# A graph attention layer's edge loop: one-hots turned on TensorE, score parts summed on VectorE, and steps staggered over three groups

## The chip, the cores and the metric

The kernel runs on one core of one Trainium2 chip. Its engines work side by side: TensorE (PE; its weight loads are listed apart as PEld), VectorE (DVE), ScalarE (ACT), GpSimd (POOL) and SyncE (SP), and 16 DMA engines. Engines wait for one another through semaphores. SBUF is the working memory, PSUM the memory into which TensorE writes.

The metric is the device time of one execution in microseconds (us). "Clock" is the share of full speed that the throttle granted to TensorE.

## The reference, cut to what matters

Four graph layers follow one another over 4096 nodes of 512 features and 65536 edges. The change touches the first, an attention layer with 8 heads:

```python
h = jnp.einsum('nc,hcf->hnf', x, W)
# ... s_src, s_dst: one number per node and head, from h
e = s_src[:, :, None] + s_dst[:, None, :]
e = jnp.where(e > 0, e, ALPHA * e)              # 0.2 * e where negative
e = jnp.where(adj[None, :, :], e, NEG_INF)      # only along edges, and from a node to itself
att = jax.nn.softmax(e, axis=-1)
out = jnp.einsum('hij,hjf->hif', att, h)
return jax.nn.softmax(out.transpose(1, 0, 2).reshape(N, H * F), axis=1)
```

## The kernel before

Edges are sorted by source node and cut into 544 tiles of 128 edges; a pair of tiles belongs to one block of 128 source nodes. Eight tiles are a group, and the loop does one group a step, 68 steps. Per group:

- GpSimd gathers, tile by tile, the row of each edge's far node: 512 features and 8 scores.
- A one-hot matrix `oh` (edge by node of the block) adds weighted rows up: `oh.T @ rows` on TensorE, two tiles into one PSUM tile `sum_ps`, which VectorE adds to `acc` ("keep").
- The turned one-hot `oh_t` (node by edge) brings each edge the numbers of its source node. They are split into three bf16 parts, so that three bf16 products add up to an f32 value in `e_ps`.

In the kernel before, the places of the edges were written to DRAM during the sort, broadcast back to all partitions by a DMA, and VectorE made `oh_t` by comparing them with the partition's number:

```python
def fetch(g):
    rows = ep.tile([P, GT, DA], F32, name="rows", bufs=4)
    for j in range(GT):
        gather(rows[:, j, :D + H], htab, s_dst[:, at(g) + j:at(g) + j + 1])
    return rows

def source_parts(g, places):
    oh_t = ep.tile([P, GT * P], BF16, name="oh_t")
    nc.vector.tensor_scalar(oh_t, places, col_i, None, op0=OP.is_equal)
    e_ps = eps.tile([P, GT, 2, H], F32, name="e_ps")
    # ... ScalarE copies the node parts of four blocks into `of`
    for j in range(GT):
        for k in range(3):
            nc.tensor.matmul(e_ps[:, j]..., oh_t[:, j * P:(j + 1) * P], of[:, j // 2, k, :],
                             start=k == 0, stop=k == 2)
    return e_ps

def weigh(j, rows):                    # two of eight heads on ScalarE, six on VectorE
    two = rows[:, j:j + 2]
    # ... ScalarE: heads VH.. of both tiles
    g = two[:, :, :VH * F].rearrange("p t (h f) -> p t h f", h=VH)
    nc.vector.tensor_mul(g, g, two[:, :, D:D + VH].unsqueeze(3).to_broadcast([P, 2, VH, F]))

for g in range(-3, groups):            # order of issue, on every engine (checks at both ends left out)
    # fetch(g + 3); fetch_places(g + 2)
    e_ps = source_parts(g + 1, places.pop(g + 1))
    ps = None
    for j in range(0, GT, 2):
        weigh(j, rows[g])
        if ps is not None:
            keep(g, j - 2, ps)
        ps = add_up(g, j, rows[g], done[g])
        if j == 2:
            u = scores(rows[g + 1], e_ps)
    done[g + 1] = weights(g + 1, rows[g + 1], u)      # also makes the one-hots
    keep(g, GT - 2, ps)
```

Both operands of `weigh` on VectorE lie in SBUF, and so do both operands of the one-hots (a row of numbers and the places `s_loc`).

## Time and profile before

Median 6524.48 us (6512.19 to 6527.41, 3 runs). The edge loop runs from 277.5 to 1048.4 us.

| In the loop, 300 to 1030 us | busy us | share of 730 us |
|---|---|---|
| TensorE | 581 | 80% |
| VectorE | 570 | 78% |
| GpSimd | 569 | 78% |
| ScalarE | 325 | 45% |
| DMA engines, mean | | 75% |

For GpSimd "busy" is the issuing of a gather, 1.080 us in the mean; the rows land later (median 3.8 us from issue to landing). One more line of the kernel before, from the view of VectorE's waits in the same stretch (engine, line, waited for: us in total, times, longest):

```profile
DVE u L707 <- DMA rows<-htab,s_dst: 4.3, 5, 2.4
```

VectorE, which takes the scores of the next group as soon as its rows have landed, waits for a landing 5 times in 66 steps.

### The profile page before, as it was taken

To read this page: it belongs to the slowest core of one execution; us is meant where nothing else is said; L and a number is where in the kernel's file an instruction comes from. 1 tells how busy PE (TensorE), PEld (TensorE's weight loads), DVE (VectorE), ACT (ScalarE), POOL (GpSimd) and SP (SyncE) were. 2 spreads that over 40 slices of the span, in tenths; PEclk is the share of its full clock that TensorE was granted. 3 is DMA by queue.
4 is the path that set the end of the run, shared out by engine and by line. 5 is a ranking of instruction groups with operands and counts; after the bars stand their busy time and mean duration, and the time that the engine had idled before them with its cause. 6 is when DMAs were issued, how large, how long until landed. Compare 5 with 4: busy or idle time off the path is not lost. (4 is left out here: it accounts for less than half of the span.)

```text
span 6523.0 us, 65629 instructions
## 1 busy us (share of the span) xinstructions
PE 5718.0 (88%) x18462; PEld 2778.4 (43%) x18462; DVE 4141.7 (63%) x7141; ACT 2937.3 (45%) x3977; POOL 3254.1 (50%) x3324
## 2 busy tenths in 40 slices
PE   6678887888779799999999999999999889978885
PEld 4366664322224344444444444444444365532221
DVE  7577778455443376676676776776766545556665
ACT  3244444300011277777777777777777533300001
POOL 1277772477760365555555555555555100037774
PEclk9899999999899899999999999999999899989998
DMA  8777775566774333333333333333333211137777
GB/s 225 182 220 214 218 215 176 162 201 203 195 214 175 125 109 103 102 98 104 101 98 105 101 98 102 103 98 106 100 98 104 82 45 62 59 106 209 210 209 243
DMA packets 399757, 926.39 MB, mean 142 GB/s; under 512 B 135926, under 2 KB 135926, under 8 KB 399382
## 3 DMA queue, kind: packets, MB, share of 16 engines
q0 software_dynamic: 230976, 721.66, 37.6%
q1 hardware_dynamic: 168406, 200.39, 9.6%
q8 instruction: 155, 2.54, 0.2%
q14 instruction: 220, 1.80, 0.1%
HBM read 818.71 MB, written 103.11 MB: 141 GB/s over the span
## 5 line engine op out<-in xcount | busy, mean ns | idle before, releaser
L438 PE MATMUL m_ps<-w_sb,h_t 128*128 128x512 f32 x4224 | 1905.9, 599 | 31.2 <-ACT h_t L957 31.2
L803 PE MATMUL sum_ps<-g,oh 128*128 128x512 f32 x2144 | 1146.9, 636 | 218.1 <-DMA g<-ztab,d_src 80.2
L438 PEld LDWEIGHTS m_ps<-w_sb,h_t 128*128 128x128 f32 x4224 | 771.1, 190 | 983.6 <-issue 791.2
L449 POOL DMA_INDIRECT qg<-qtab,eg x528 | 504.0, 954 | 990.6 <-ACT h_t L957 845.7
L449 POOL DMA_INDIRECT g<-ztab,d_src x528 | 501.4, 950 | 866.4 <-issue 811.6
L459 DVE TENSOR_TENSOR acc<-acc,sum_ps 128x512 f32 x800 | 550.2, 688 | 546.4 <-PE sum_ps L803 541.4
L803 PEld LDWEIGHTS sum_ps<-g,oh 128*128 128x128 f32 x2144 | 336.9, 191 | 1015.4 <-DVE acc L459 388.5
L449 POOL DMA_INDIRECT g<-ytab,s_dst x544 | 536.9, 987 | 353.2 <-DMA ytab<-acc 185.6
L914 POOL DMA_INDIRECT eg<-aug,d_eid x528 | 569.0, 1078 | 242.4 <-issue 131.0
L449 POOL DMA_INDIRECT rows<-htab,s_dst x544 | 585.9, 1077 | 204.9 <-issue 138.9
L957 ACT COPY h_t<-tr_ps 128x512 f32<-128x512 f32 x528 | 283.6, 589 | 777.6 <-PE tr_ps L955 777.6
L735 PE MATMUL sum_ps<-rows,oh 128*128 128x261 f32 x2176 | 551.5, 410 | 60.3 <-PE sum_ps L735 41.2
L449 POOL DMA_INDIRECT pg<-ptab,eg x528 | 508.7, 963 | 160.9 <-issue 160.6
L735 PEld LDWEIGHTS sum_ps<-rows,oh 128*128 128x128 f32 x2176 | 427.3, 202 | 163.3 <-PE sum_ps L735 66.3
L967 PE MATMUL small_ps<-z,oh 128*128 128x512 f32 x1056 | 477.8, 595 | 8.4 <-DVE z L1027 8.4
L1006 DVE TENSOR_TENSOR z<-m_ps,b_bc 128x512 f32<-128x512 f32 x132 | 91.3, 692 | 467.3 <-PE m_ps L438 467.3
L459 DVE TENSOR_TENSOR acc<-acc,small_ps 128x512 f32 x528 | 361.1, 684 | 31.8 <-PE small_ps L967 4.3
L1165 ACT ACTIVATE acc<-acc,dis 128x512 f32<-128x512 f32 x32 | 19.7, 706 | 671.2 <-DVEq L464 671.2
L1027 DVE TENSOR_TENSOR z<-z,t 128x1024 f32<-128x1024 f32 x264 | 310.4, 1217 | 8.2 <-ACTq L464 4.8
L992 DVE TENSOR_TENSOR z<-m_ps,b_bc 128x512 f32<-128x512 f32 x132 | 91.3, 692 | 352.6 <-PE m_ps L438 352.6
L967 PEld LDWEIGHTS small_ps<-z,oh 128*128 128x128 f32 x1056 | 201.5, 191 | 263.7 <-issue 221.9
L955 PEld LDWEIGHTS tr_ps<-ident,pg 128*128 128x128 f32 x2112 | 248.0, 142 | 151.1 <-issue 120.0
(248 smaller groups left out, 8389.5 us busy)
## 6 DMA issues: line engine op xcount, KB each, us to landing
aug<-row SPq DMA_DIRECT2D x32, 560.0 KB, 3.9
places<-loc_rows SPq DMA_DIRECT2D x68, 256.0 KB, 3.8
xt<-in_x_dram SPq DMA_DIRECT2D x16, 1024.0 KB, 5.7
row<-in_edge_attr_dram SPq DMA_DIRECT2D x32, 512.0 KB, 6.6
x<-xt SPq DMA_DIRECT2D x16, 1024.0 KB, 4.3
xt<-x SPq DMA_DIRECT2D x16, 1024.0 KB, 7.5
rows<-htab,s_dst POOLq DMA_INDIRECT x544, 3.8
g<-ytab,s_dst POOLq DMA_INDIRECT x544, 3.7
```

The lines of the kernel that those rows point to most:

```text
L438: nc.tensor.matmul(ps, h_t[:, k, :], w_sb[:, k0 + k, :], start=start and k == 0, stop=stop and k == KC - 1)
L449: nc.gpsimd.indirect_dma_start(out=dst_ap, out_offset=None, in_=table, in_offset=bass.IndirectOffsetOnAxis(ap=idx, axis=0))
L459: nc.vector.tensor_add(into, into, ps)
L735: nc.tensor.matmul(ps[:, c, :HW], oh[:, j + k, :], rows[:, j + k, c * HW:(c + 1) * HW], start=k == 0, stop=k == 1)
L803: nc.tensor.matmul(ps, oh[:, j + k, :], g[:, j + k, :], start=k == 0, stop=k == pair - 1)
L914: nc.gpsimd.indirect_dma_start(out=eg[:, j // 2, (j % 2) * HALF:(j % 2 + 1) * HALF], out_offset=None, in_=aug.rearrange("e c -> (e c)").un ...
L955: nc.tensor.transpose(h_ps[:, k, :], h[:, j, k * P:(k + 1) * P], ident)
L957: nc.scalar.copy(h_t, h_ps)
L967: nc.tensor.matmul(ps, oh, m, start=True, stop=True)
L992: nc.vector.tensor_add(zz[:, 0, :], ps, b2_bc)
L1006: nc.vector.tensor_add(zz[:, 1, :], ps, b2_bc)
L1027: nc.vector.tensor_mul(mz[:, j:j + 2], mz[:, j:j + 2], t[:, j:j + 2])
```

## The change

The intent: no broadcast through DRAM and no comparison on VectorE; TensorE turns the one-hots that exist anyway; one product of 48 columns in place of three of 16 that accumulate; VectorE adds the three parts; and the work of a step is dealt out over three groups, so that no engine waits for a result that was only just begun.

```diff
-            def fetch_places(g): ...          # DMA broadcast of the places
+            def turn(oh):
+                made = []
+                for j in range(0, GT, 4):
+                    t_ps = eps.tile([P, 4, P], F32, name="t_ps")
+                    for k in range(4):
+                        nc.tensor.transpose(t_ps[:, k, :], oh[:, j + k, :], ident)
+                    made.append(t_ps)
+                return made
+            def turned(g, made):
+                oh_t = ep.tile([P, GT, P], BF16, name="oh_t")
+                for j, t_ps in enumerate(made):
+                    nc.scalar.copy(oh_t[:, 4 * j:4 * j + 4, :], t_ps)
                 ...
-                e_ps = eps.tile([P, GT, 2, H], F32, name="e_ps")
+                e_ps = eps.tile([P, GT, 3, 2 * H], F32, name="e_ps")
                 for j in range(GT):
-                    for k in range(3): nc.tensor.matmul(..., of[:, j // 2, k, :], start=k == 0, stop=k == 2)
+                    nc.tensor.matmul(..., of[:, j // 2].rearrange("p k c -> p (k c)"), start=True, stop=True)
             def scores(rows, e_ps):
+                near = ep.tile([P, GT, 2 * H], F32, name="near")
+                nc.vector.reduce_sum(near, e_ps.rearrange("p t k c -> p t c k"), axis=AX.X)
                 ...
+            # order of a step, with w = weigh, k = keep, a = add_up:
+            #   turn(g+1); w0; a0; w2; k6 of g-1; turned(g+1); a2; w4; k0; one_hots(g+2);
+            #   source_parts(g+1); a4; scores(g+1); w6; k2; a6; weights(g+1); k4
```

ScalarE's share of the weighing (`weigh_last`) became a function of its own and is issued one pair ahead. The one-hots get three buffers. Nothing else in the kernel is touched, but that the cast and the store of the places leave the sort.

More of the change, by code (lines that the diff above doesn't have):

```diff
@@ L86 @@
                    allow_small_or_imprecise_dtypes=True)
-    col_i = const.tile([P, 1], F32, name="col_i")
-    nc.gpsimd.iota(col_i, pattern=[[0, 1]], base=0, channel_multiplier=1,
-                   allow_small_or_imprecise_dtypes=True)
     acc = keep_pool.tile([P, NB, DA], F32, name="acc")
@@ L114 @@
     aug = dram.tile([E + 1, EA], F32, name="aug")
-    loc_rows = dram.tile([G * P, P], BF16, name="loc_rows")
     x1 = dram.tile([N, D], F32, name="x1")
@@ L305, in by_order @@
         placed(s_loc, loc)
-        low_p = pool.tile([P, G, P], BF16, name="low_p")
-        nc.vector.tensor_copy(low_p, loc)
-        nc.sync.dma_start(loc_rows.rearrange("(g p) c -> p g c", p=P), low_p)
         new = pool.tile([P, G, P], F32, name="new")
@@ L439, in product, with one_hots @@
                              start=start and k == 0, stop=stop and k == KC - 1)
-    def one_hots(pool, loc, t0, n):
-        oh = pool.tile([P, n, P], F32, name="oh")
+    def one_hots(pool, loc, t0, n, bufs=None):
+        oh = pool.tile([P, n, P], F32, name="oh", bufs=bufs)
         nc.vector.tensor_tensor(oh, row_i.unsqueeze(1).to_broadcast([P, n, P]),
@@ L683, in fetch @@
                 return rows
-            def fetch_places(g):
-                places = ep.tile([P, GT * P], BF16, name="places", bufs=3)
-                nc.sync.dma_start(places, loc_rows[at(g):at(g) + GT].rearrange("t c -> (t c)").partition_broadcast(P))
-                return places
-            def source_parts(g, places):
-                oh_t = ep.tile([P, GT * P], BF16, name="oh_t")
-                nc.vector.tensor_scalar(oh_t, places, col_i, None, op0=OP.is_equal)
-                e_ps = eps.tile([P, GT, 2, H], F32, name="e_ps")
+            def turn(oh):
[10 more added lines that the diff above has]
+                    nc.scalar.copy(oh_t[:, 4 * j:4 * j + 4, :], t_ps)
                 of = ep.tile([P, GT // 2, 3, 2 * H], BF16, name="of")
@@ L698, in source_parts @@
                     nc.scalar.copy(of[:, j // 2], node3[:, ds(b, 1)].rearrange("p b k c -> p (b k) c"))
+                return oh_t, of
+            def source_parts(oh_t, of):
+                e_ps = eps.tile([P, GT, 3, 2 * H], F32, name="e_ps")
                 for j in range(GT):
-                    for k in range(3):
-                        nc.tensor.matmul(e_ps[:, j].rearrange("p c h -> p (c h)"), oh_t[:, j * P:(j + 1) * P],
-                                         of[:, j // 2, k, :], start=k == 0, stop=k == 2)
+                    nc.tensor.matmul(e_ps[:, j].rearrange("p k c -> p (k c)"), oh_t[:, j, :],
+                                     of[:, j // 2].rearrange("p k c -> p (k c)"), start=True, stop=True)
                 return e_ps
             def scores(rows, e_ps):
+                near = ep.tile([P, GT, 2 * H], F32, name="near")
+                nc.vector.reduce_sum(near, e_ps.rearrange("p t k c -> p t c k"), axis=AX.X)
                 u = ep.tile([P, GT, H], F32, name="u")
-                nc.vector.tensor_add(u, e_ps[:, :, 0, :], rows[:, :, D:D + H])
+                nc.vector.tensor_add(u, near[:, :, :H], rows[:, :, D:D + H])
                 nc.vector.scalar_tensor_tensor(u, u, 0.2, u, op0=OP.mult, op1=OP.max)
-                nc.vector.tensor_sub(u, u, e_ps[:, :, 1, :])
+                nc.vector.tensor_sub(u, u, near[:, :, H:])
                 nc.vector.tensor_scalar(u, u, SAFE_RANGE + 10.0, None, op0=OP.min)
@@ L718, in weights, with weigh_last @@
                                      s_new[:, at(g):at(g) + GT].unsqueeze(2).to_broadcast([P, GT, H]))
-                return one_hots(ep, s_loc, at(g), GT)
-            def weigh(j, rows):
+            def weigh_last(j, rows):
                 two = rows[:, j:j + 2]
@@ L727, in weigh @@
                                              scale=two[:, k, D + h:D + h + 1])
+            def weigh(j, rows):
+                two = rows[:, j:j + 2]
                 g = two[:, :, :VH * F].rearrange("p t (h f) -> p t h f", h=VH)
@@ L742, in keep @@
                 nc.vector.tensor_add(into, into, ps[:, :, :HW])
-            rows, places, done = {}, {}, {}
-            for g in range(-3, groups):
+            rows, ohs, sums = {}, {}, {}
+            for g in range(-3, groups + 1):
                 now = lambda k: 0 <= k < groups
@@ L748, in run @@
                     rows[g + 3] = fetch(g + 3)
+                if now(g + 1):
+                    made = turn(ohs[g + 1])
+                if now(g):
+                    weigh(0, rows[g])
+                    sums[0] = add_up(g, 0, rows[g], ohs[g])
+                    weigh_last(2, rows[g])
+                    weigh(2, rows[g])
+                if now(g - 1):
+                    keep(g - 1, 6, sums.pop(6))
+                    del rows[g - 1], ohs[g - 1]
+                if now(g + 1):
+                    parts = turned(g + 1, made)
+                if now(g):
+                    sums[2] = add_up(g, 2, rows[g], ohs[g])
+                    weigh_last(4, rows[g])
+                    weigh(4, rows[g])
+                    keep(g, 0, sums.pop(0))
                 if now(g + 2):
-                    places[g + 2] = fetch_places(g + 2)
+                    ohs[g + 2] = one_hots(ep, s_loc, at(g + 2), GT, 3)
                 if now(g + 1):
-                    e_ps = source_parts(g + 1, places.pop(g + 1))
-                ps = None
-                for j in range(0, GT, 2):
-                    if now(g):
-                        weigh(j, rows[g])
-                        if ps is not None:
-                            keep(g, j - 2, ps)
-                        ps = add_up(g, j, rows[g], done[g])
-                    if j == 2 and now(g + 1):
-                        u = scores(rows[g + 1], e_ps)
+                    e_ps = source_parts(*parts)
+                if now(g):
+                    sums[4] = add_up(g, 4, rows[g], ohs[g])
                 if now(g + 1):
-                    done[g + 1] = weights(g + 1, rows[g + 1], u)
+                    u = scores(rows[g + 1], e_ps)
                 if now(g):
-                    keep(g, GT - 2, ps)
-                    del rows[g], done[g]
+                    weigh_last(6, rows[g])
+                    weigh(6, rows[g])
+                    keep(g, 2, sums.pop(2))
+                    sums[6] = add_up(g, 6, rows[g], ohs[g])
+                if now(g + 1):
+                    weights(g + 1, rows[g + 1], u)
+                    weigh_last(0, rows[g + 1])
+                if now(g):
+                    keep(g, 4, sums.pop(4))
         run()
```

## The prediction

> **What bounds the kernel now.** I first asked how much of the span the change can touch at all, then what sets the pace there. The page gives 6523.0 us for the profiled execution. The instructions that write or read `rows` start at 277.5 us and end at 1048.4 us, so layer 0's edge loop is about 770 us, 12% of the span. It has 544 tiles in groups of 8, thus 68 steps. Everything else stays as it is (only one small cast and one store leave the sort before it). The loop's middle, cut by stretches (start:end, length, busy time and instructions of PE, PEld, DVE, ACT and POOL, granted TensorE clock, DMA share, GB/s):
>
> ```profile
> 300.00:1030.00 730.00, 581.01 (x3659) 454.99 (x3657) 569.97 (x987) 325.19 (x1452) 568.51 (x527) 0.95 0.75 216
> 609.40:612.60 3.20, 3.20 (x9) 2.51 (x8) 1.65 (x6) 0.00 (x0) 2.57 (x3) 0.50 0.75 232
> 885.00:896.00 11.00, 8.28 (x56) 6.55 (x56) 8.97 (x16) 5.21 (x24) 8.56 (x9) 1.00 0.78 224
> ```
>
> No engine looks full: TensorE 80%, VectorE 78%, GpSimd 78%. The groups of instructions in that stretch (busy us, mean ns, then idle before and what ended it) say more:
>
> ```profile
> L449 POOL DMA_INDIRECT rows<-htab,s_dst x527 | 568.9, 1080 | 160.6 <-issue 134.1 <-PE sum_ps L735 9.4 <-DMA rows<-htab,s_dst 5.2
> L735 PE MATMUL sum_ps<-rows,oh 128*128 128x261 f32 x2099 | 531.7, 409 | 57.5 <-PE sum_ps L735 40.4 <-issue 7.6
> L742 DVE TENSOR_TENSOR acc<-acc,sum_ps 128x522 f32 x263 | 182.6, 694 | 149.3 <-PE sum_ps L735 148.8
> L701 PE MATMUL e_ps<-of,oh_t 128*128 128x16 bf16 x1560 | 49.6, 170 | 90.4 <-DVE oh_t L693 90.4
> ```
>
> GpSimd is busy 568.9 us and idle 160.6 us: together 729.5 of 730. Its 527 idle pieces are 0.305 us each, the same after every gather, so it is never without a gather to issue: one takes 1.385 us (1.080 + 0.305), eight take 11.1 us, which is the step. A gather that nothing disturbs takes 0.945 us, with the pause 1.25 us, so eight need at least 10.0 us. What stretches them shows in one undisturbed step (start, length, engine; granted clock 1.00):
>
> ```profile
> 885.50 0.54 DVE L693 TENSOR_SCALAR oh_t<-places,col_i 128x1024 bf16<-128x1024 bf16 x1
> 885.96 1.81 DVE L729 TENSOR_TENSOR rows<-rows 128x768 f32<-128x768 f32 x2
> 886.10 1.63 POOL L449 DMA_INDIRECT rows<-htab,s_dst  x1 [0.31 <-issue]
> 886.10 0.76 PE L701 MATMUL e_ps<-of,oh_t 128*128 128x16 bf16 x24 [1.42 <-DVE oh_t L693]
> 887.00 3.76 PE L735 MATMUL sum_ps<-rows,oh 128*128 128x261 f32 x16
> 889.04 0.70 DVE L742 TENSOR_TENSOR acc<-acc,sum_ps 128x522 f32 x1 [1.27 <-PE sum_ps L735]
> 891.62 3.76 PE L735 MATMUL sum_ps<-rows,oh 128*128 128x261 f32 x16 [0.85 <-PE sum_ps L735]
> 893.66 0.70 DVE L742 TENSOR_TENSOR acc<-acc,sum_ps 128x522 f32 x1 [0.66 <-PE sum_ps L735]
> ```
>
> The gather at 886.10 starts while VectorE's weighing (two operands in SBUF) runs and takes 1.63 us in place of 0.95. The other seven of that step take 0.95. So 7 x 1.25 + 1.93 = 10.7 us, exactly the step (oh_t starts at 885.50 and 896.20). At the same time VectorE and TensorE chase each other round a ring of 10.7 us: turned one-hots 0.60, their products 0.90, first pair of sums 2.04, keep 0.62, scores 0.87, weighing 1.09, next pair 2.04, keep 0.61, weights and one-hots 1.32, last keep 0.61. There are two limits near each other: the ring (10.7) and GpSimd (10.0 plus what VectorE holds up).
>
> **What the Trainium skill says.** "SBUF — State Buffer", Who interferes with whom: a VectorE instruction with two SBUF inputs contends with a GpSimd instruction that reads SBUF; the page thinks that descriptor generation is spared. The trace agrees with the first (1.63 against 0.95 us, and in the mean 1.080 over all gathers) and not with the second. "Perfetto Trace Analysis", DMA Instruction — SWDGE (GPSIMD): the end shown is that of the descriptors, not of the data; the trace's median from issue to landing is 3.8 us against 0.95 us shown. "TensorE: Matmul & The Clock Gate", Part 1: TensorE falls to half clock after idle windows; in 609.4 to 612.6 the granted clock is 0.50, and a product that starts every 0.22 us elsewhere starts every 0.43 us. "VectorE: DVE Perf Modes", the perf-mode tier table: a reduction has no fast mode.
>
> **The change, part by part, per step.**
> - VectorE loses the comparison for turned one-hots: 0.54 us. It gains the sum of a score's three parts: 384 elements in, 128 out, out of PSUM. The kernel's 512-element reduction takes 0.686 us, a strided 256-element one 0.781 us, so 0.55 to 0.9 us (estimate). The other instructions stay. By start-to-start intervals: four weighings 3.6, four keeps 2.4, one-hots 1.13, weights 0.19, scores 1.0, new sum 0.65: 9.0 us. Balance: about zero.
> - TensorE gains 8 transposes. The ones of layer 2 with the same shape (128x128 f32) start every 0.11 us: 0.9 us. It loses 16 of 24 small products, which start every 0.025 us: -0.4 us and no more, even if the wider ones take somewhat longer. The sums stay at 32 x 0.22 = 7.0 us. Total 8.3 us.
> - ScalarE gains two copies of 128x512 out of PSUM, 0.587 us each by layer 2's: 1.2 us on top of 325/66 = 4.9 us. At 6.1 us it bounds nothing.
> - DMA loses 68 broadcasts of 256 KB, 23 of 216 GB/s. These sit on another queue than the gathers, and no wait of weight was for them.
> - The order: turned one-hots, scores and last keep lie across three groups, so the ring of 10.7 us opens. What remains in TensorE's and VectorE's new order: the fourth pair needs keep 2 (for its PSUM buffer), then fourth pair 1.75, transposes 0.9, two pairs 3.5, score products 0.5, new sum 0.65, scores 1.0, weighing 0.95, keep 0.6, hand-overs 0.4: about 10.2 us, 0.5 less than before.
> - GpSimd issues the same 544 gathers: 10.0 us and the same VectorE instructions to hold them up. It becomes the bound, and this is the floor: 68 x (11.1 - 10.0) = 75 us at the very most, 6450 us.
>
> How much hold-up is left decides the result. A gather that meets a running weighing or one-hot waits for its end less 0.125 us. If they met by chance, per gather (4 x 0.825^2 / 2 + 1.085^2 / 2) / 11 = 0.18 us, thus 1.4 us a step. Before it was 8 x 0.135 = 1.1 us. So the new step lies between 10.4 (well placed) and 11.5 (by chance), and 12.3 if each of four gathers walks into a weighing. I walked one GpSimd-bound step by hand, with the scores starting when the last gather lands: the 4th, 6th, 7th and 8th gather were held 0.70, 0.65, 0.20 and 0.75 us, which gives 12.3; with a landing 0.5 us later they mostly passed. I choose 10.9 us, as the ring still sets part of the phase: 68 x -0.2 = -14 us.
>
> **The rivals.**
> - The wait at the turned one-hots was all that held the loop, and it goes: TensorE's 90.4 us and VectorE's 148.8 us become gain. For it: these waits are real. Against it: GpSimd has only 1.1 us a step to give. Even in full this is 6450 us.
> - VectorE's and GpSimd's instructions meet worse than before, as GpSimd now leads and the scores wait for its landing: 11.5 to 12.3 us a step, 6550 to 6605 us. For it: the hand-walk, and ScalarE and the small VectorE instructions now crowd the middle of a step. Against it: the early steps of this trace, where VectorE does wait for landings, still take 10.6 to 11.3.
> - TensorE, waiting for gathers in longer pieces, drops to half clock more often: each such window of 3.4 us costs 1.7 us, and the ring then exceeds GpSimd's pace: 11.3 us, 6540 us. For it: 0.94 to 0.95 mean clock now with gaps of 1.4 us. Against it: more work on TensorE (8.3 of about 11 us), spread better.
> - The extra work binds: ScalarE's copies come late and hold the score products. Against it: TensorE has two pairs, 3.5 us, to work at meanwhile.
>
> **Range and chances.** Around 6510 us: 6460 if gathers pass nearly freely (10.15 a step), 6575 if they are held 0.75 us a step more than now. Two per cent is 130 us or 1.9 us a step. Faster by that is under the floor of 10.0; slower needs 13 us a step, past the worst of the above. So within 2% has 0.95.
>
> **What would show it.** Right: the groups' view shows GpSimd's busy and idle again adding to the whole loop, 0.305 us after each gather; the wait of the score products on VectorE's comparison is gone; VectorE waits for the landing of `rows` before the scores; the loop takes 700 to 780 us, the rest unchanged within 5 us. Wrong: gathers with pauses over 0.31 us (GpSimd waits for buffers, so TensorE or VectorE binds), a gather that alone takes less than 0.94 us, or a new sum of scores over 1.2 us.

## The result, and the profile after

Median 6542.06 us (6537.70 to 6549.40, 4 runs) against 6524.23 us: 0.3% slower. The ratio is 1.0032, 95% interval 1.0014 to 1.0049; by the 2% rule this counts as the same. A ratio here is the mean time of one kernel's fast runs over that of the other's fast runs of the same rounds, so it isn't quite the ratio of the two medians.

The loss lies in the loop. The last instruction on `rows` starts at 1070.8 us in place of 1048.4, while the first starts 2.5 us earlier; what follows takes 5477 us after and 5475 us before. The loop's middle, in the view of stretches (columns as in the prediction):

```profile
300.00:1030.00 730.00, 575.76 (x3036) 473.37 (x3037) 559.89 (x953) 400.15 (x1526) 575.18 (x509) 0.94 0.68 186
```

The groups of instructions in the same stretch:

```profile
L441 POOL DMA_INDIRECT rows<-htab,s_dst x509 | 576.1, 1132 | 155.1 <-issue 125.2 <-PE sum_ps L741 16.2 <-DMA rows<-htab,s_dst 6.1
L741 PE MATMUL sum_ps<-rows,oh 128*128 128x261 f32 x2024 | 515.2, 404 | 154.8 <-issue 154.8
...
L748 DVE TENSOR_TENSOR acc<-acc,sum_ps 128x522 f32 x255 | 177.4, 696 | 85.6 <-PE sum_ps L741 83.5 <-DVE rows L720 1.4
...
L691 ACT CAST oh_t<-t_ps 128x512 bf16<-128x512 f32 x126 | 69.0, 588 | 62.9 <-PE t_ps L683 62.6
...
L708 DVE TENSOR_REDUCE near<-e_ps 128x128 f32<-128x384 f32 x63 | 35.1, 558 | 7.9
```

Three things are to be seen. The wait at the comparison (90.4 us of TensorE before) is gone, and VectorE's wait for sums fell from 148.8 to 83.5 us. The new pieces cost what was expected: 0.588 us for a copy, 0.558 us for the sum of three parts. But in 730 us GpSimd issued 509 gathers in place of 527: the mean gather grew from 1.080 to 1.132 us, and busy time and pauses again fill the stretch (576.1 + 155.1 = 731.2). VectorE's waits say who now leads:

```profile
DVE acc L748 <- PE sum_ps L741: 83.5, 83, 2.3
DVE u L710 <- DMA rows<-htab,s_dst: 67.9, 46, 2.9
```

VectorE waits 46 times for the landing of the rows; before, 5 times. So the scores of a group now stand behind GpSimd's last gather. And why gathers are longer shows in the timeline (start, length, engine, line):

```profile
656.29 0.95 DVE L735 TENSOR_TENSOR rows<-rows 128x768 f32<-128x768 f32 x1
...
656.61 1.45 POOL L441 DMA_INDIRECT rows<-htab,s_dst  x1 [0.30 <-DMA rows<-htab,s_dst]
...
658.58 1.82 DVE L735 TENSOR_TENSOR rows<-rows 128x768 f32<-128x768 f32 x2
...
659.62 1.61 POOL L441 DMA_INDIRECT rows<-htab,s_dst  x1 [0.30 <-issue]
...
660.93 0.95 DVE L735 TENSOR_TENSOR rows<-rows 128x768 f32<-128x768 f32 x1
...
661.53 1.17 POOL L441 DMA_INDIRECT rows<-htab,s_dst  x1 [0.30 <-issue]
```

Each gather here starts inside a weighing and is longer by about what is left of that weighing. I put all 544 gathers of both traces down to the VectorE instruction that was running 0.13 us after their start, and counted those longer than 0.945 us by over 0.02 us. Before, 112 were held by a weighing (61 us lost in all) and 28 by a one-hot (10 us); after, 185 and 64 (84 and 16 us). Everything above 0.945 us a gather sums to 71.8 us before and 100.4 us after: 28.6 us more, beside 24.6 us more span of the two profiled runs.

This agrees with a bound on GpSimd, but it doesn't prove it. GpSimd filled its time before as well.

### The profile page after: what moved, and what is told of

Same layout as the page of the kernel before. It is cut to its first block, busy times and chain, and to the rows that moved or that the text cites. A ratio compares the mean times of both kernels' runs of the same rounds, so it can differ in the third digit from the quotient of the medians.

```text
span 6547.6 us, 64534 instructions
## 1 busy us (share of the span) xinstructions
PE 5733.3 (88%) x17918; PEld 2816.8 (43%) x17918; DVE 4148.9 (63%) x7140; ACT 3029.5 (46%) x4113; POOL 3284.5 (50%) x3323
## 5 line engine op out<-in xcount | busy, mean ns | idle before, releaser
L441 POOL DMA_INDIRECT rows<-htab,s_dst x544 | 614.5, 1130 | 204.4 <-issue 135.0
```

The source lines that it names most:

```text
L441: nc.gpsimd.indirect_dma_start(out=dst_ap, out_offset=None, in_=table, in_offset=bass.IndirectOffsetOnAxis(ap=idx, axis=0))
```

## The experiments

A step is taken from the first and last start of the instruction that writes the weights, divided by 67: for the kernel before (1038.4 - 292.1) / 67 = 11.14 us, after (1060.3 - 289.8) / 67 = 11.50 us.

| run | median us | ratio to before | step us |
|---|---|---|---|
| before | 6520.8 to 6524.5 | 1 | 11.14 |
| after | 6542.06 | 1.0032 | 11.50 |
| e1_weights_psum | 6474.93 | 0.9927 | 10.45 |
| e2_both_psum | 6451.07 | 0.9890 | 10.06 |
| e3_before_psum | 6552.84 | 1.0047 | 11.57 |
| e4_new_ops_old_order | 6777.17 | 1.0390 | 14.89 |
| e5_old_ops_new_order | 6570.90 | 1.0073 | 11.80 |
| e6_pair_twice | 6540.15 | 1.0030 | 11.41 |
| e7_copy_unused | 6542.93 | 1.0034 | 11.48 |
| e8_seven_gathers | 6447.95 | 0.9886 | 10.00 |
| e9_before_seven | 6522.49 | 1.0003 | 11.05 |
| e10_after_seven | 6433.19 | 0.9862 | 9.83 |

Each has 4 runs; the 95% intervals are within 0.0022 of the ratios.

The theory: after the change GpSimd sets the pace, and its gathers are held by VectorE instructions with two operands in SBUF. The rivals: TensorE and VectorE set the pace and GpSimd only fills its time; TensorE's windows of half clock cost it; the added work costs it.

### Taking the second SBUF operand away (e1, e7, e2)

e1 copies the weights to a free corner of the PSUM tile of the scores, and the weighing reads them there:

```diff
+                w_ps[g] = whole[:, GT * 6 * H:GT * 7 * H]...      # behind e_ps, same PSUM tile
             def weights(g, rows, u):
                 nc.vector.tensor_mul(rows[:, :, D:D + H], u, ...)
+                nc.vector.tensor_copy(w_ps[g], rows[:, :, D:D + H])
             def weigh(g_, j, rows):
-                nc.vector.tensor_mul(g, g, two[:, :, D:D + VH].unsqueeze(3)...)
+                nc.vector.tensor_mul(g, g, w_ps[g_][:, j:j + 2, :VH].unsqueeze(3)...)
```

> The changed kernel with the weights also copied to PSUM, so that a weighing has one operand in SBUF and one in PSUM. Theory (GpSimd is the bound, and its gathers are held by VectorE instructions with two SBUF operands): the 184 gathers held by weighings pass; mean gather from 1.130 to about 0.97 us, step from 11.5 to about 10.3 us, loop about 75 us shorter than in the changed kernel, 6470 us. Rival (TensorE and VectorE set the pace and GpSimd only fills its time): VectorE has one more instruction of 0.2 us, so 6540 to 6560 us.

The kernel took 6474.93 us, 67 us less than the changed one, and the step 10.45 us. The mean gather fell to 0.999 us; the mean weighing is 0.947 us, against 0.953, so it is hardly faster; it lets gathers through. The control e7 makes the same copy and doesn't use it:

```diff
-                nc.vector.tensor_mul(g, g, w_ps[g_][:, j:j + 2, :VH].unsqueeze(3)...)
+                nc.vector.tensor_mul(g, g, two[:, :, D:D + VH].unsqueeze(3)...)
```

> Control for e1_weights_psum: the copy of the weights to PSUM is made but the weighings still read both operands from SBUF. Theory (the second SBUF operand holds the gathers): nothing gained, mean gather 1.09 to 1.15 us, 6525 to 6560 us. Rival (the extra instruction or the changed tile only shifted the phase between the engines): 6470 to 6490 us, as e1.

6542.93 us, as the changed kernel. So it is the place of the operand and not an added instruction or a shifted phase. e2 moves the one-hots' places to PSUM too:

```diff
+                nc.vector.tensor_copy(l_ps[g + 2], s_loc[:, at(g + 2):at(g + 2) + GT])
-                    ohs[g + 2] = one_hots(ep, s_loc, at(g + 2), GT, 3)
+                    ohs[g + 2] = one_hots(ep, l_ps[g + 2] if g >= 0 else s_loc[:, at(g + 2):], 0, GT, 3)
```

> As e1_weights_psum, and the one-hots read their row places out of PSUM too. Theory: no gather is held any more, mean 0.95 us; the step is the larger of 10.0 us (eight gathers) and the ring of TensorE and VectorE, which I worked out as 10.2 us and which has two small copies more: 10.0 to 10.5 us, 6440 to 6480 us. Rival (ring binds): no gain, 6540 to 6570 us.

6451.07 us, the lower part of what was expected. The gathers of e1, e7 and e2, from the view of groups:

```profile
L441 POOL DMA_INDIRECT rows<-htab,s_dst x514 | 513.7, 999 | 156.6 <-issue 125.2 <-PE sum_ps L746 13.4 <-DVE u L718 8.8
```
```profile
L441 POOL DMA_INDIRECT rows<-htab,s_dst x510 | 576.0, 1129 | 155.4 <-issue 122.8 <-PE sum_ps L746 18.6 <-DMA rows<-htab,s_dst 7.9
```
```profile
L441 POOL DMA_INDIRECT rows<-htab,s_dst x527 | 499.5, 948 | 160.6 <-issue 123.4 <-PE t_ps L683 8.8 <-PE sum_ps L749 8.8
```

The mean of e2 is 0.948 us: hardly a gather is held any more (1.8 us over all 544), and the step of 10.06 us is close to eight times 1.253 us. This kernel is faster than both, by 1.1% than the one before and by 91 us than the changed one. It passed the comparison with the reference; as that comparison turns out below to miss wrong rows, this is weak evidence, but the edit only copies values.

### The same in the kernel before (e3)

The same two operands are moved to PSUM, in the old order:

```diff
+                nc.vector.tensor_copy(w_ps[g], rows[:, :, D:D + H])
+                nc.vector.tensor_copy(l_ps[g + 1], s_loc[:, at(g + 1):at(g + 1) + GT])
-                return one_hots(ep, s_loc, at(g), GT)
+                return one_hots(ep, l_ps[g] if g > 0 else s_loc[:, at(g):], 0, GT)
```

> The kernel before with the same two operands moved to PSUM, old order and old operations. Theory (before, the ring of 10.7 us at full clock, plus windows of half clock, set the pace beside GpSimd, and GpSimd had room for 0.7 us of hold-up a step): gathers pass at 0.95 us and now show pauses over 0.31 us, waiting for buffers, but the time stays within 20 us of before: 6505 to 6545 us. Rival (GpSimd alone bound the kernel before): step 10.0 to 10.3 us, 6450 to 6475 us.

6552.84 us: no gain, but 32 us of loss, 8 us beyond what I had allowed. The mean gather is 0.952 us, and now GpSimd waits, as the waits of 300 to 970 us show:

```profile
POOL rows L449 <- PE sum_ps L743: 87.3, 50, 2.8
```

It waits for TensorE to give a buffer of rows back: freed, GpSimd would be faster than the ring of VectorE and TensorE. The two copies (0.23 and 0.17 us) lie in this ring and would make up most of the loss, 68 x 0.40 = 27 us (an estimate; no run adds the copies alone). I had left them out of the expected time.

### Seven gathers in place of eight (e8, e9, e10)

This takes a gather from GpSimd and leaves VectorE and TensorE as they are: every eighth tile is loaded by SyncE's DMA queue, the same bytes from fixed rows. The rows are wrong on purpose. The comparison with the reference passed all the same, so it is blind to this edit and says nothing here.

```diff
-                for j in range(GT):
+                for j in range(GT - 1):
                     gather(rows[:, j, :D + H], htab, s_dst[:, at(g) + j:at(g) + j + 1])
+                nc.sync.dma_start(rows[:, GT - 1, :D + H], htab[g % NB * P:(g % NB + 1) * P])
```

e9 is this edit on the kernel before, e10 on the changed one, e8 on e2.

> The kernel before with every eighth tile loaded by the DMA queue of SyncE from fixed rows (same bytes, wrong result on purpose): GpSimd issues seven gathers a step, VectorE and TensorE do exactly the same as before. Theory (before, the closed ring of VectorE and TensorE with its half-clock windows set the pace): pauses over 0.31 us appear, the time stays within 20 us of before, 6500 to 6535 us. Rival (GpSimd, busy or pausing for all of the loop, set the pace before): the step falls by one gather of 1.38 us, 6425 to 6450 us.

> The same edit on the changed kernel (wrong result on purpose). Theory (after the change GpSimd's held gathers set the pace and the opened ring takes about 10.0 us): seven gathers of 1.43 us are 10.1 us, so the step falls from 11.5 to 10.1 to 10.5 us, 6450 to 6480 us. Rival (the change lengthened the ring, GpSimd only follows): 6530 to 6550 us.

In the kernel before nothing happens: 6522.49 us, ratio 1.0003 (0.9985 to 1.0021). GpSimd, which had seemed full, now stands idle, in this view of its waits from 300 to 940 us:

```profile
POOL rows L449 <- issue: 91.1, 299, 0.3
POOL rows L449 <- PE sum_ps L736: 89.5, 57, 3.2
```

The changed kernel loses 109 us, to 6433.19 us, more than I expected (6450 to 6480): the step falls to 9.83 us, where VectorE no longer waits for landings and the ring of TensorE and VectorE sets the pace. All of its waits from 300 to 940 us:

```profile
DVE acc L749 <- PE sum_ps L742: 47.2, 65, 0.8
DVE u L711 <- DVE near L709: 1.5, 6, 0.4
DVE acc L749 <- DVE rows L721: 1.0, 3, 0.3
```

GpSimd still looks full here (501.5 us busy and 139.5 us of pauses in 640 us), as it did in the kernel before. What tells a leader from a follower is whether others wait for its result: VectorE waited 46 times for a landing in the changed kernel, and never here. So the change did open the ring, from 11.1 to about 9.8 us, and GpSimd took its place as the bound.

> From e2_both_psum; every eighth tile is loaded by the DMA queue of SyncE from fixed rows, the same bytes, so that GpSimd issues seven gathers a step (wrong result on purpose). Theory (e2 runs at GpSimd's floor of eight gathers, 10.0 us a step): the floor falls to 8.75 us and the step to the ring of TensorE and VectorE, which must lie below 10.0: 9.2 to 9.9 us, 6395 to 6445 us, with pauses over 0.31 us between some gathers. Rival (ring and floor happen to be equal, or DMA binds): 6445 to 6460 us, as e2.

This expectation missed. e8 took 6447.95 us, 3 us less than e2, as the rival had it (ring and floor equal, or DMA binds): step 10.00 us, and GpSimd now with pauses for TensorE:

```profile
POOL rows L441 <- PE sum_ps L750: 87.4, 61, 1.9
```

The DMA engines aren't the limit: in 300 to 970 us they moved 209 GB/s, and 218 in e10 (300 to 940 us). So the ring of e2, which has two copies more than that of e10, takes 10.0 us, just what eight free gathers take. In e2 both limits lie at the same place, and a further gain would have to move both.

### The order and the operations apart (e4, e5)

e4 takes the new operations in the old order:

```diff
-                    e_ps = source_parts(g + 1, places.pop(g + 1))
+                    e_ps = source_parts(*turned(g + 1, turn(ohs[g + 1])))
                 # ... the old loop over the pairs
+                    ohs[g + 2] = one_hots(ep, s_loc, at(g + 2), GT, 3)
```

> One part of the change alone: turned one-hots by TensorE and ScalarE, one product and the sum by VectorE, in the order of before. Theory: the ring stays closed and gets longer: transposes 0.9, two copies 1.3 and products 0.55 in place of keep 0.6, comparison 0.6 and products 0.9 (+0.65), new sum +0.55: about 1.2 us a step, 6580 to 6610 us, and gathers with pauses over 0.31 us, as GpSimd waits for buffers. Rival (the new operations cost nothing, the order alone made the change slower): 6510 to 6530 us.

6777.17 us: the ring does get longer, but by 3.8 us a step and not by 1.2. One step of it in the timeline:

```profile
622.78 1.09 PE L691 MATMUL t_ps<-ident,oh 128*128 128x128 f32 x8 [0.30 <-DVE oh L444]
...
623.53 1.07 ACT L699 CAST oh_t<-t_ps 128x512 bf16<-128x512 f32 x2 [3.41 <-PE t_ps L691]
...
627.14 0.24 PE L710 MATMUL e_ps<-of,oh_t 128*128 128x48 bf16 x2 [0.71 <-ACT of L703]
...
627.24 6.56 PE L745 MATMUL sum_ps<-rows,oh 128*128 128x261 f32 x16
```

From the start of the transposes to the first sums it takes 4.5 us; I had reckoned 2.75. I had counted ScalarE's two copies but not its four copies of node parts behind them, for each of which the products wait. And 16 sums take 6.56 us in place of 3.76, as TensorE is at half clock for part of the time (mean granted clock 0.86 from 300 to 1270 us). e5 is the other half, the old operations in the new order:

```diff
-                    made = turn(ohs[g + 1])
+                    places[g + 2] = fetch_places(g + 2)
-                    parts = turned(g + 1, made)
+                    parts = turned(g + 1, places.pop(g + 1))      # VectorE compares, as before
-                nc.vector.reduce_sum(near, e_ps.rearrange("p t k c -> p t c k"), axis=AX.X)
```

> The other part alone: the order of three staggered groups, with the broadcast, the comparison by VectorE and three products. Theory: the ring is open, GpSimd binds with its gathers held by the same weighings and one-hots as in the changed kernel: no pauses over 0.31 us, mean gather 1.10 to 1.14 us, 6525 to 6555 us. Rival (the added work of TensorE and ScalarE costs the changed kernel its gain): 6470 to 6500 us.

6570.90 us, slower than expected by 16 us and slower than the changed kernel. It is bound as that one is: VectorE waits 101.4 us for landings (300 to 970 us), GpSimd's busy time and pauses (580.5 + 150.5 us) fill the 730 us, and its mean gather is longer still:

```profile
L448 POOL DMA_INDIRECT rows<-htab,s_dst x494 | 580.5, 1175 | 150.5 <-issue 120.3 <-PE sum_ps L741 14.6 <-DVE u L714 4.6
```

So the new operations aren't what cost the change its gain: without them the new order is slower. How many gathers are held depends on where the instructions happen to meet, and I couldn't reckon it well: the mean gather is 1.175 us, against the 1.10 to 1.14 expected.

### Is it the clock? (e6)

The third pair's products are computed twice into the same PSUM tile, in TensorE's idle time; the result is the same.

```diff
                     sums[4] = add_up(g, 4, rows[g], ohs[g])
+                    add_up(g, 4, rows[g], ohs[g], sums[4])
```

> The changed kernel with the third pair's products computed twice into the same PSUM tile: 1.75 us more TensorE work a step in a place where it stands idle, same result. Theory (TensorE is off the bound, its half-clock windows cost nothing): within 8 us of the changed kernel, 6535 to 6555 us. Rival A (idle TensorE falls to half clock and that costs the time): fewer half-clock windows and 15 to 40 us faster. Rival B (TensorE's added work is what made the change slower): up to 68 x 1.75 = 119 us slower.

6540.15 us against 6542.06: no difference beyond the spread. The mean granted clock of the loop rose from 0.94 to 1.00, with 80 us more TensorE work in the stretch:

```profile
300.00:1030.00 730.00, 655.39 (x3588) 547.18 (x3587) 562.24 (x963) 401.55 (x1536) 574.01 (x513) 1.00 0.67 188
```

A gain by the clock and a loss by the work could cancel in such a run, so look at who waits. VectorE's wait for landings grew from 67.9 to 101.7 us:

```profile
DVE u L710 <- DMA rows<-htab,s_dst: 101.7, 58, 3.6
```

What TensorE gave was spent on waiting for GpSimd. So both rivals fall: in the changed kernel neither the half-clock windows nor TensorE's work set the time.

## Why the prediction was right or wrong

The measured 6542 us lies in the range (6460 to 6575), and the class, within 2%, is right. The middle value had the wrong sign: 14 us gained was predicted, 18 us lost was measured. So the range held because it was wide, and the account of the limits did better than the number.

- **That GpSimd becomes the bound, with a floor of 10.0 us a step:** right. e10 shows the bound, and e2 the floor (10.06 us; 6451 us, where the prediction had put 6450 at the very least).
- **That VectorE instructions with two SBUF operands hold the gathers:** right, shown by e1, e2 and the control e7.
- **That GpSimd's full time was a limit of the kernel before, beside the ring:** half right. The ring alone set the pace; with one gather less nothing changes (e9). GpSimd only looked full. My reading, which no run tests by itself, is that a gather that comes too early meets the same weighing and is held until it ends, so that GpSimd is stretched to the ring's step. "Eight take 11.1 us, which is the step" was a result of the ring and not a second limit.
- **The ring opened to about 10.2 us:** right in direction; 9.83 us was measured (e10), 10.00 us with two copies more (e8).
- **The costs part by part:** the sum of parts 0.558 us (0.65 reckoned), copies 0.588 us (0.587), the balance on VectorE about zero.
- **"I choose 10.9 us, as the ring still sets part of the phase":** this is the step that failed. With the scores behind the landing, GpSimd led in most steps, and the hold-up was 68 x 8 gathers of 0.185 us, that is 1.48 us a step, where the value by chance in the prediction was 1.4 us and the choice amounted to 0.9. The prediction's own rival, 11.5 us a step, is what came (11.50 us). The time it gave for it (6550 us) is 8 us above the measured one. Two of the prediction's figures are loose: 10.0 and 1.4 make 11.4, where it wrote 11.5, and its 10.4 (well placed) has no sum behind it.
- **The rival that the wait at the comparison was all that held the loop:** wrong. That wait of 90.4 us is gone, and the loop is longer.
- **The rival of the clock:** wrong as a cost, since e6 removes nearly all of the half clock and gains nothing.
- **The rival of the extra work:** wrong in this order, since without the new operations the loop is slower (e5); in the old order they cost 3.8 us a step (e4).
- **"The loop takes 700 to 780 us":** missed; from the first to the last instruction on `rows` it took 796 us. The rest did stay within 5 us.

What was argued and not shown: why in the new order 249 gathers are held by weighings and one-hots and in the old one 140. It was seen that scores now begin at a landing and gathers therefore start at a set distance from the weighings, but no run varied that distance alone.

## What to carry to other kernels

An engine whose busy time and pauses fill a loop may still only follow: see whether others wait for its results, take a piece of its work away, and see whether the time moves. When gathers from GpSimd run beside VectorE, a VectorE operand placed in PSUM in place of SBUF can be worth more than a reordering, as it lets gathers through without making VectorE faster. And when a change removes a wait, reckon what the next bound loses to contention before counting the wait as gain.

## What the Trainium skill lacked or had wrong

- "SBUF — State Buffer", Who interferes with whom: the page infers that a `tensor_tensor` with both inputs in SBUF leaves descriptor generation alone. Here it holds GpSimd's indirect gathers: mean 1.132 us in the changed kernel, 0.948 us once the second operand lies in PSUM, the longest 1.974 us. The page's rule for GpSimd instructions that read SBUF would fit, as a gather has its indices there; that this is the read that waits isn't shown.
- The same page gives an amount for a DMA from GpSimd beside a `tensor_copy`, and none for a gather beside a `tensor_tensor`. In the traces of both kernels a gather is held only if the VectorE instruction runs when it starts, for what is left of that instruction less about 0.125 us; two-operand instructions of 0.22 to 0.28 us added at most 0.01 us in the mean.
- No page has the price of an indirect gather on GpSimd: 0.945 us for 128 rows of 2080 bytes, and 0.305 us to the next, so 1.25 us each where no VectorE instruction holds it.
- "TensorE: Matmul & The Clock Gate", Part 1, ties half clock to an idle window of about 3.4 us, and in a second case to short idle times without a length. In the kernel before TensorE's clock fell to half 23 times in the loop, for 3.41 us each, and in the 3.41 us before each fall no pause between products was over 1.42 us. The page doesn't say either that this can cost nothing: with the clock brought from 0.94 to 1.00 the time stayed (6542 and 6540 us).
